# Token lists earlier and gathered tokens turned through DRAM for twelve expert jobs

## The chip, the cores and the metric

The kernel runs on one core of one Trainium2 chip. The metric is the device time of one execution in microseconds (us); it is given as the median of the runs. A profile is one further execution, recorded instruction by instruction.

## The reference

The computation is a transformer block with a mixture of experts, on 16 sequences of 256 tokens with 256 channels, all in float32. Attention has 16 heads of 64 channels; its result is added to `x`. Then each of 8 experts chooses its 512 best of the 4096 tokens (by the softmax over experts of a gate), and the chosen tokens go through that expert's two-layer network and are added back with the gate as weight:

```
shift = silu(t) @ W_ada.T + b_ada
h = ln(x, ln1_g, ln1_b) + shift
q, k, v = heads(h @ Wqkv.T);  q = ln(q, qn_g, qn_b);  k = ln(k, kn_g, kn_b)
x = x + (softmax(q @ k.T / sqrt(64)) @ v) @ Wout.T
tok = x.reshape(-1, 256)
gate = softmax(tok @ Wgate.T)
vals, idx = top_k(gate.T, 512)                  # for each of the 8 experts
g = ln(tok[idx], mlp_g, mlp_b)
y = gelu(g @ fc1s[e].T + b1s[e])                # 256 -> 1024
y = y @ fc2s[e].T + b2s[e]                      # 1024 -> 256
tok[idx] += y * vals                            # for every expert
```

## The kernel before

The span has three parts. The attention stage (0 to about 800 us) treats the 16 sequences in an order that is written out by hand. In it the turned keys and probabilities already go through DRAM: VectorE turns 32x32 blocks (L746, L832), SyncE's queue writes the blocks to DRAM (`away`) and reads them back in four transfers in another order of blocks (`back`). Then a first routing (about 800 to 850 us) chooses tokens, and an expert stage follows (about 850 us to the end).

The expert stage has 16 jobs of 256 tokens each. Jobs 0 to 7 are the eight experts with a first routing over 30 of the 32 tiles of 128 tokens; jobs 8 to 15 are the experts again with a second routing over all 32 tiles, which runs beside jobs 1 to 6. Job 0 and the lists of jobs 0 and 1 belong to the ordered part. From job 1 on a loop `for k in range(1, len(jobs))` goes through 16 slots a job; the order of its calls is the order of the instructions on each engine.

For the running job `a` (number k):

- slots 0 to 7: `up(s)` makes one eighth of the hidden layer on TensorE (L1268), `gelu(s)` applies the activation on ScalarE (L1275); `weigh` in slot 7 multiplies the bias with the tokens' weights on VectorE (L1292)
- slots 8 to 15: `down` (L1284), four slots for each 128 tokens, with `finish` on VectorE (L1295) and `scatter` (L1301) in slots 11 and 15. The scatter is an indirect DMA from GpSimd's queue (POOL) that adds rows of the output in DRAM.

For the next job `new` (k + 1), in the same slots:

- slot 5 (`LIST_AT`): `list_matmul` (L1224) turns the token list out of one-hot matrices, `take` (L1233, L1235) brings it to SBUF as indices and weights, and `gather` (L1240) fetches the normalised token rows from DRAM into `xg`, as two indirect DMAs on POOL
- slot 14 (`TURN_AT`): `transposes` (L1249) turns the gathered tokens with four TensorE matmuls into PSUM tile `px`, and `evict` (L1256) brings them to `xT` with two affine ScalarE passes (gain and bias of the layer norm)

For the job after that (`far`, k + 2): `lay_out` is a generator. It has 15 steps: the first makes `gives` (L1192, L1197), each of the 14 others two or three of the 32 one-hot matrices on VectorE (L1216). One step is taken a slot, in slots 6 to 15 of one job and 0 to 4 of the next. At the end of a job, `far.load()` puts the expert's weights on SyncE's queue: `w2` and `w1`, 1 MB each, and `b2`, 128 KB. Their buffers come free when job k has used its own.

Job 8 is the first of the second routing. In loop k = 7 its one-hots are made in slots 0 to 5, and its list in slot 7 (`LATE_AT`, the name `late`).

The second routing is a search by two bits a round. `compare_three` (L1042) counts on VectorE how many gates reach three candidates, `count_three` (L1049) adds the counts over partitions on TensorE, and `choose_bits` (L1055 to L1064) decides. A round stands in every fifth slot; `masks`, `scans`, `place` and `split` follow in loop k = 6.

Buffers that matter: `xg` has 5 ("xs"), `xT` 2 ("hT"), the one-hot tiles 2 ("kT"), and the PSUM tiles of `px` and of the routing's counts share 3 ("mm").

Of the kernel before, what the change touches and what calls it, by code (L numbers as in the profile page):

```python
# [9 lines left out]
F32 = mybir.dt.float32  # L10
I32 = mybir.dt.int32
BF16 = mybir.dt.bfloat16
AF = mybir.ActivationFunctionType
# [5 lines left out]
P = 128  # L19
# [8 lines left out]
DC = D // P  # L28
# [3 lines left out]
KL = KC // 2  # L32
CAPL = CAP // 2
NV = 5
SQ = 32
QB = P // SQ
# [3 lines left out]
LN1_G, LN1_B, B_ADA, MLP_G, MLP_B = 0, 2, 4, 6, 8  # L40
# [4 lines left out]
class Plan:  # L45
# [7 lines left out]
    def step(self, place, engine, took, run, needs=(), makes=(), tiles=(), mode=0, lag=0.1):  # L53
        k = len(self.steps)
        self.steps.append((place, engine, took, run, needs, tiles, mode, lag))
        for m in makes:
            self.makers.setdefault(m, []).append(k)
# [7 lines left out]
def kernel(  # L65
# [14 lines left out]
    nc = tc.nc  # L80

    const = ctx.enter_context(tc.tile_pool(name="const", bufs=1))
    dram = ctx.enter_context(tc.tile_pool(name="dram", bufs=1, space=DRAM))
# [6 lines left out]
    vec = const.tile([P, NVEC], F32, name="vec")  # L90
# [432 lines left out]
    if True:  # L523
        attw = ctx.enter_context(tc.tile_pool(name="attw", bufs=1))
        seq = ctx.enter_context(tc.tile_pool(name="seq", bufs=2))
        work = ctx.enter_context(tc.tile_pool(name="work", bufs=2))
# [22 lines left out]
        class Shift:  # L549
            def __init__(self):  # L550
                self.pa = {}
# [75 lines left out]
        class First:  # L627
# [22 lines left out]
            def evict(self):  # L650
                b = self.b
                hTs[b] = seq.tile([P, DC, N], F32, tag="hT", name=f"hT{b}")
                for c in range(DC):
                    nc.scalar.activation(
                        hTs[b][:, c, :], self.pt[:, c, :], AF.Identity,
                        bias=bias1[:, c, b : b + 1],
                        scale=vec[:, LN1_G + c : LN1_G + c + 1],
                    )
# [12 lines left out]
        class Group:  # L671
# [74 lines left out]
            def turn(self, kb):  # L746
                if self.t == 0:
                    kb.append(work.tile([P, QB, TB, HP // 2, SQ], F32, tag="pb", bufs=3, name="kb"))
                nc.vector.transpose(
                    kb[0][:, :, self.t],  # L750
                    self.qk.rearrange("p (h q d) -> p q h d", q=QB, d=SQ),
                )

            def away(self, kb):
                self.blocks = dram.tile([QB, SQ, QB, N], F32, tag="blocks", bufs=4, name="kblocks")
                nc.sync.dma_start(
                    self.blocks.rearrange("k d q n -> (k d) (q n)"),
                    kb[0].rearrange("p q t h m -> p (q t h m)"),
                )

            def back(self):
                kT = self.keys()[:, self.g - 2].rearrange("p k t h m -> p k (t h m)")
                for q in range(QB):
                    nc.sync.dma_start(
                        kT[bass.ts(q, SQ)], self.blocks[:, :, q].rearrange("k d n -> d k n")
                    )

            def affine(self):
                kT = self.keys()[:, self.g - 2].rearrange("p k t h m -> p (k t h m)")
                nc.scalar.activation(  # L770
                    kT, kT, AF.Identity,
                    bias=vec[:, KN_B : KN_B + 1], scale=vec[:, KN_G : KN_G + 1],
                )
# [398 lines left out]
        class Job:  # L1172
            def __init__(self, e, routing, tiles):
                self.e, self.routing, self.tiles = e, routing, tiles
                self.oh = None

            def load(self):


                e = self.e  # L1180
                self.w2 = seq.tile([P, FC, D], F32, tag="oT", name="w2")
                nc.sync.dma_start(self.w2, fc2T[e].rearrange("(f p) d -> p f d", p=P))
                self.w1 = seq.tile([P, DC, DD], F32, tag="v", bufs=2, name="w1")
                nc.sync.dma_start(self.w1, fc1T[e].rearrange("(c p) f -> p c f", p=P))
                self.b2 = moe.tile([P, D], F32, tag="b2", bufs=2, name="b2")
                nc.sync.dma_start(self.b2, b2s[:, bass.ts(e, D)].to_broadcast([P, D]))
# [66 lines left out]
            def evict(self):  # L1253
                self.xT = seq.tile([P, DC, CAPL], F32, tag="hT", name="xT")
                for c in range(DC):
                    nc.scalar.activation(  # L1256
                        self.xT[:, c, :], self.px[:, c, :], AF.Identity,
                        bias=vec[:, MLP_B + c : MLP_B + c + 1],
                        scale=vec[:, MLP_G + c : MLP_G + c + 1],
                    )  # L1260
                self.hid = seq.tile([P, FC, CAPL], F32, tag="qT", name="hid")
                self.y = work.tile([P, KL, D], F32, tag="pr", bufs=PRB, name="y")
                self.ph, self.py = {}, {}

            def up(self, f):
                self.ph[f] = ps.tile([P, CAPL], F32, tag="sc", bufs=4, name="ph")
                for c in range(DC):
                    nc.tensor.matmul(  # L1268
                        self.ph[f], self.w1[:, c, bass.ts(f, P)], self.xT[:, c, :],
                        start=(c == 0), stop=(c == DC - 1),  # L1270
                    )

            def gelu(self, f):
                k = B1 + self.e * FC + f
                nc.scalar.activation(  # L1275
                    self.hid[:, f, :], self.ph[f], AF.Gelu_apprx_tanh,
                    bias=vec[:, k : k + 1], scale=1.0,
                )

            def down(self, i, a=0, b=FC):  # L1280
# [51 lines left out]
        for b in range(B):  # L1332
# [16 lines left out]
            for (g, t), p in GROUP.items():  # L1349
                p += base  # L1350
                a = Group(b, g, t)
                n = (b, g, t)
# [23 lines left out]
            for d in range(HP // 2):  # L1376
                a = Quad(b, d)
                p = base + d * QUAD
                g = d // 2
                n = (b, d)  # L1380
                po = ("po", 0) + n
                for i in range(2):
                    q = p + 3 * i
                    m = n + (i,)
                    sums, pb, prT, blocks = ("sums",) + m, ("pb",) + m, ("prT",) + m, ("blocks",) + m
# [20 lines left out]
            for t in range(TB):  # L1406
                a = Tail(b, t)
                p = base + TAIL[t]
                n = (b, t)
# [55 lines left out]
        for n in range(2):  # L1465
            a = jobs[n]
            k = top + 10 + 20 * n
# [4 lines left out]
            for i in range(6):  # L1472
                name, took, by = {"D": ("DVE", 0.81, nc.vector), "P": ("POOL", 1.4, nc.gpsimd), "A": ("ACT", 3.5, nc.scalar)}[who[i]]
# [13 lines left out]
        k = top + 30  # L1487
# [9 lines left out]
        for k in plan.order(PLACES):  # L1497
            plan.steps[k][3]()

        LIST_AT, TURN_AT, LATE_AT = 5, 14, 7  # L1500
        SLOTS = 2 * FC

        def second_routing():
# [9 lines left out]
        def lay_out(job):  # L1513

            job.gives()
            for a in list(range(0, 18, 2)) + list(range(18, NT, 3)):
                yield
                job.onehot(a, a + (2 if a < 18 else 3))

        rest = second_routing()  # L1520
        last = len(jobs) // 2 - 2
        jobs[2].load()
        parts = iter(())
        for k in range(1, len(jobs)):
            a = jobs[k]
            new = jobs[k + 1] if k + 1 < len(jobs) else None
            far = jobs[k + 2] if k + 2 < len(jobs) else None
            late = k == last + 1
            for s in range(SLOTS):
                for step in next(rest, ()):  # L1530
                    step()
                if late and s == 0:
                    new.gives()
                if late and s < 6:
                    new.onehot(6 * s, 6 * s + 6)
                if new and s == (LATE_AT if late else LIST_AT):
                    for _ in () if late else parts:
                        pass
                    new.list_matmul(0, NT)
                    new.take()  # L1540
                    new.gather()
                    if k == 1:
                        jobs[0].scatter(by_end[1])
                if new and s == TURN_AT:
                    new.transposes()
                    new.evict()
                if not late and s < LIST_AT:
                    next(parts, None)
                if far and k != last and s > LIST_AT:
                    if s == LIST_AT + 1:  # L1550
                        parts = lay_out(far)
                    next(parts)
                if s < FC:
                    a.up(s)
                    a.gelu(s)
                    if s == FC - 1:
                        a.weigh()
                else:
                    i, q = divmod(s - FC, 4)
                    a.down(i, 2 * q, 2 * q + 2)  # L1560
                    if q == 3:
                        a.finish(i)
                        a.scatter(i)
            if far:
                far.load()
# [50 lines left out]
```

## Time and profile before

| | |
|---|---|
| time, median of 3 runs | 1104.54 us (1104.27, 1104.54, 1107.28) |
| profiled execution | 1106.04 us, of which its span is 1104.2 us |
| TensorE clock granted, mean | 0.99 |
| expert loop, k = 1 to 15 | 865.61 to 1094.80 us of the span |
| one job of k = 1 to 5 | 15.4 us |
| job k = 6 | 17.0 us |
| one job of k = 7 to 14 | 15.1 us |

The names of the engines in the profile: PE is TensorE (PEld its weight loads), DVE VectorE, ACT ScalarE, POOL GpSimd, SP SyncE (SPq its DMA issues). Times in a line of the timeline are the start in us of the span and the length in us. What stands in brackets is how long the engine was idle before the instruction and which instruction or DMA, by tile and line, ended the wait.

### The profile page before, as it was taken

The numbers are of one execution on the slowest core, as the hardware profiler recorded it, in microseconds if no ns is written. First come the engines' busy times: TensorE is split into PE (matmuls) and PEld (weight loads), VectorE is DVE, ScalarE is ACT, GpSimd is POOL, SyncE is SP. The second block draws the span as 40 slices with busy tenths as digits, with TensorE's granted clock in tenths as the row PEclk, the third lists the DMA queues.
The fourth block names the chain that finished last, engine by engine and source line by source line (L and its number), as shares of the span: only waits on it lengthen the run. The fifth ranks groups of instructions, "written<-read, shape, count | busy, mean of one in ns | idle before, by whom it ended". The sixth has DMA issues, their size and how long they took to land. (4 is left out here: it accounts for less than half of the span.)

```text
span 1104.2 us, 18872 instructions
## 1 busy us (share of the span) xinstructions
PE 1070.6 (97%) x5835; PEld 714.8 (65%) x5835; DVE 778.9 (71%) x2201; ACT 596.1 (54%) x1656; POOL 616.2 (56%) x997
## 2 busy tenths in 40 slices
PE   7999999999999999999899999999988999999996
PEld 4555656566565655656465655656767888888885
DVE  6657888777778777786678787676568488654540
ACT  2768666565766566566557667576522333322331
POOL 3766776776676665675657666565411233333332
PEclk9999999999999999999999999999999999999998
DMA  6013998785888787796787778895130456555661
GB/s 211 1 39 123 277 259 237 230 255 166 248 260 227 226 246 234 201 260 211 211 251 227 228 224 240 243 256 179 63 102 20 113 189 200 170 162 175 196 201 19
DMA packets 147539, 209.20 MB, mean 189 GB/s; under 512 B 15088, under 2 KB 122864, under 8 KB 147440
## 3 DMA queue, kind: packets, MB, share of 16 engines
q1 hardware_dynamic: 139520, 197.71, 60.0%
q0 software_dynamic: 6144, 8.39, 4.1%
q10 hardware_dynamic: 1776, 1.90, 0.5%
q8 instruction: 47, 0.77, 0.3%
q14 instruction: 52, 0.43, 0.1%
HBM read 121.96 MB, written 85.98 MB: 188 GB/s over the span
## 5 line engine op out<-in xcount | busy, mean ns | idle before, releaser
L683 PE MATMUL pm<-wq,hT 128*128 128x512 f32 x768 | 360.4, 605 | 5.0 <-DVE qk L716 2.8
L822 POOL TENSOR_SCALAR pr<-pr,sums 128x256 f32<-128x256 f32 x512 | 237.1, 481 | 112.2 <-DVE sums L818 92.9
L811 ACT ACTIVATE pr<-sc,nmax 128x256 f32<-128x256 f32 x512 | 238.0, 480 | 97.5 <-DVE nmax L802 80.3
L683 PEld LDWEIGHTS pm<-wq,hT 128*128 128x128 f32 x768 | 137.3, 192 | 146.1 <-issue 131.1
L103 POOL TENSOR_TENSOR ss<-ss,neghalf 128x8 f32<-128x8 f32 x128 | 210.5, 1645 | 10.6
L802 DVE TENSOR_REDUCE nmax<-sc 128x2 f32<-128x512 f32 x256 | 165.3, 676 | 16.9 <-PE sc L794 16.3
L832 DVE STREAM_TRANSPOSE pb<-pr 128x512 f32<-128x512 f32 x224 | 149.9, 690 | 18.5 <-POOL pr L822 13.6
L794 PE MATMUL sc<-kT,qT 64*128 64x256 f32 x1024 | 135.4, 397 | 0.0
L881 PE MATMUL po<-prT,v 128*64 128x256 f32 x1024 | 127.6, 388 | 1.1 <-DVE gates L950 1.1
L700 DVE TENSOR_REDUCE ss<-sq 128x8 f32<-128x512 f32 x128 | 86.0, 672 | 47.3 <-ACT sq L696 46.8
L794 PEld LDWEIGHTS sc<-kT,qT 64*128 64x128 f32 x1024 | 92.8, 188 | 40.8 <-issue 25.4
L696 ACT ACTIVATE sq<-pm 128x512 f32<-128x512 f32 x128 | 76.9, 603 | 77.3 <-PE pm L683 75.9
L1301 POOL DMA_INDIRECT out<-y,idx x32 | 51.2, 1601 | 119.8 <-DVE y L1295 66.9
L1268 PE MATMUL ph<-xT,w 128*128 128x256 f32 x512 | 117.6, 383 | 0.0
L907 PE MATMUL pw<-wo,oT 128*128 128x256 f32 x512 | 116.6, 381 | 0.3 <-DVE qk L716 0.3
L1284 PE MATMUL py<-w,hid 128*128 128x256 f32 x512 | 116.3, 380 | 0.0
L716 DVE TENSOR_TENSOR qk<-pm,ss 128x512 f32<-128x512 f32 x128 | 87.0, 681 | 36.9 <-POOL ss L103 35.9
L907 PEld LDWEIGHTS pw<-wo,oT 128*128 128x128 f32 x512 | 96.0, 190 | 23.2 <-issue 9.4
L811 ACT ACTIVATION_READ_ACCUMULATOR pr<-sc,nmax 128x1 f32 x512 | 107.6, 210 | 0.0
L881 PEld LDWEIGHTS po<-prT,v 128*64 128x64 f32 x1024 | 67.1, 137 | 61.5 <-issue 21.1
L1275 ACT ACTIVATE hid<-ph,vec 128x256 f32<-128x256 f32 x128 | 60.4, 474 | 84.2 <-PE ph L1268 76.3
L1284 PEld LDWEIGHTS py<-w,hid 128*128 128x128 f32 x512 | 95.6, 190 | 12.8
(140 smaller groups left out, 1132.6 us busy)
## 6 DMA issues: line engine op xcount, KB each, us to landing
blocks<-pb SPq DMA_DIRECT2D x112, 512.0 KB
prT<-blocks SPq DMA_DIRECT2D x448, 128.0 KB
w<-in_fc2T SPq DMA_DIRECT2D x16, 1024.0 KB
w<-in_fc1T SPq DMA_DIRECT2D x16, 1024.0 KB
kblocks<-kb SPq DMA_DIRECT2D x28, 512.0 KB
kT<-kblocks SPq DMA_DIRECT2D x112, 128.0 KB
out<-tok SPq DMA_DIRECT2D x32, 128.0 KB
xn_dram<-tn SPq DMA_DIRECT2D x32, 128.0 KB
```

Of the source, the lines that this page charges most:

```text
L103: nc.gpsimd.tensor_tensor(dst, src, neghalf[:, : src.shape[1]], ALU.pow)
L683: nc.tensor.matmul(self.pm, hTs[self.b][:, c, bass.ts(self.t, P)], wq[:, c, bass.ts(self.g, GW)], start=(c == 0), stop=(c == DC - 1),)
L716: engine.tensor_tensor(self.qk.rearrange("p (h d) -> p h d", d=HD), src.rearrange("p (h d) -> p h d", d=HD), self.ss[:, 1, :].unsqueeze(2) ...
L794: nc.tensor.matmul(self.sc[i, j][:, t, :], qTs[self.b][rows, hp, bass.ts(t, P)], keys[rows, hp] if direct else keys[rows, hp // 4, hp % 4] ...
L802: nc.vector.tensor_reduce(self.nmax[i, j], self.sc[i, j], AX.X, ALU.max, negate=True)
L811: nc.scalar.activation(self.pr[i, j][:, t, :], self.sc[i, j][:, t, :], AF.Exp, bias=self.nmax[i, j][:, t : t + 1], scale=1.0, accum_out=se ...
L822: nc.gpsimd.tensor_scalar(self.pr[i, j][:, t, :], self.pr[i, j][:, t, :], self.sums[i][:, 1, j, t : t + 1], 1.0, ALU.mult, ALU.mult,)
L832: nc.vector.transpose(self.pb[i][:, :, :, j].rearrange("p k c t n -> p t k c n"), self.pr[i, j].rearrange("p t (k c m) -> p t k c m", c=TB ...
L881: nc.tensor.matmul(self.po[j * HD : (j + 1) * HD, i, :], vs[self.b][:, c, bass.ts(4 * self.d + 2 * i + j, HD)], prT[:, j, c] if self.b in ...
L907: nc.tensor.matmul(self.pw, oTs[self.b][:, hp // 2, self.t, hp % 2, :], wo[:, hp, :], start=(hp == 0), stop=(hp == HP - 1),)
L1268: nc.tensor.matmul(self.ph[f], self.w1[:, c, bass.ts(f, P)], self.xT[:, c, :], start=(c == 0), stop=(c == DC - 1),)
L1284: nc.tensor.matmul(self.py[i], self.hid[:, f, bass.ts(i, P)], self.w2[:, f, :], start=(f == 0), stop=(f == FC - 1),)
```

## The change

The list of the next job moves from slot 5 to slot 0. Two jobs keep theirs: loop k = 1 (slot 5) and loop k = 7 (slot 7). In loops k = 2 to 6 and 8 to 14, twelve in all, the gathered tokens are no longer turned by TensorE. In slot 6 VectorE turns them in 32x32 blocks into `xb` (two instructions), SyncE writes `xb` to DRAM (256 KB) and reads it back in four transfers of 64 KB in the order of blocks that makes `xT`; in slot 12 ScalarE applies the two affine passes in place. The tokens of such an `xT` lie in another order, so `up` reads it through a view, and `gelu` writes the hidden layer through one that puts the tokens in their old order. The one-hots now stand in slots 1 to 15, and loop k = 1 takes two steps a slot, in slots 6 to 15.

```diff
+            def turn(self):
+                self.xb = work.tile([P, QB, DC, KL, SQ], F32, tag="prT", bufs=4, name="xb")
+                for i in range(KL):
+                    nc.vector.transpose(
+                        self.xb[:, :, :, i].rearrange("p q c m -> p c q m"),
+                        self.xg[:, i].rearrange("p (c q d) -> p c q d", c=DC, d=SQ),
+                    )
+
+            def away(self):
+                self.blocks = dram.tile([QB, SQ, QB, P], F32, tag="xblocks", bufs=2, name="xblocks")
+                nc.sync.dma_start(
+                    self.blocks.rearrange("k d q n -> (k d) (q n)"),
+                    self.xb.rearrange("p q c i m -> p (q c i m)"),
+                )
+
+            def back(self):
+                self.xT = seq.tile([P, QB, DC, KL, SQ], F32, tag="hT", name="xT")
+                xT = self.xT.rearrange("p k c i m -> p k (c i m)")
+                for q in range(QB):
+                    nc.sync.dma_start(
+                        xT[bass.ts(q, SQ)], self.blocks[:, :, q].rearrange("k d n -> d k n")
+                    )
+
+            def affine(self):
+                for c in range(DC):
+                    xT = self.xT[:, :, c].rearrange("p k i m -> p k (i m)")
+                    nc.scalar.activation(
+                        xT, xT, AF.Identity,
+                        bias=vec[:, MLP_B + c : MLP_B + c + 1],
+                        scale=vec[:, MLP_G + c : MLP_G + c + 1],
+                    )
+                self.outputs()
...
                     nc.tensor.matmul(
-                        self.ph[f], self.w1[:, c, bass.ts(f, P)], self.xT[:, c, :],
+                        self.ph[f], self.w1[:, c, bass.ts(f, P)],
+                        self.xT[:, :, c].rearrange("p k i m -> p k (i m)") if self.exchanged else self.xT[:, c, :],
                         start=(c == 0), stop=(c == DC - 1),
                     )
...
+                dst, src = self.hid[:, f, :], self.ph[f]
+                if self.exchanged:
+                    dst = dst.rearrange("p (i k m) -> p k i m", i=KL, m=SQ)
+                    src = src.rearrange("p (k i m) -> p k i m", i=KL, m=SQ)
                 nc.scalar.activation(
-                    self.hid[:, f, :], self.ph[f], AF.Gelu_apprx_tanh,
-                    bias=vec[:, k : k + 1], scale=1.0,
+                    dst, src, AF.Gelu_apprx_tanh, bias=vec[:, k : k + 1], scale=1.0
                 )
...
-        LIST_AT, TURN_AT, LATE_AT = 5, 14, 7
+        LIST_AT, TURN_AT, LATE_AT = 0, 14, 7
+        EXCHANGE = {6: ("turn", "away", "back"), 12: ("affine",)}
...
             late = k == last + 1
+            list_at = LATE_AT if late else 5 if k == 1 else LIST_AT
+            exchanged = k > 1 and not late
             for s in range(SLOTS):
...
-                if new and s == (LATE_AT if late else LIST_AT):
+                if new and s == list_at:
...
-                if new and s == TURN_AT:
+                if new and exchanged:
+                    new.exchanged = True
+                    for what in EXCHANGE.get(s, ()):
+                        getattr(new, what)()
+                elif new and s == TURN_AT:
                     new.transposes()
                     new.evict()
-                if not late and s < LIST_AT:
+                if not late and s < list_at:
                     next(parts, None)
-                if far and k != last and s > LIST_AT:
-                    if s == LIST_AT + 1:
+                if far and k != last and s > list_at:
+                    if s == list_at + 1:
                         parts = lay_out(far)
-                    next(parts)
+                    for _ in range(2 if k == 1 else 1):
+                        next(parts, None)
```

More of the change, by code (lines that the diff above doesn't have):

```diff
@@ L1175, in __init__ @@
                 self.oh = None
+                self.exchanged = False
             def load(self):
@@ L1260, in evict, with outputs @@
                     )
+                self.outputs()
[27 more added lines that the diff above has]
+                    )
+                self.outputs()
+            def outputs(self):
                 self.hid = seq.tile([P, FC, CAPL], F32, tag="qT", name="hid")
```

## The prediction

> **What bounds the kernel now.** I read the page's busy times first, then a table of windows cut at the jobs' first `up` matmuls, then the timeline of one job, then the waits and landings of the gathers. On the page:
>
> ```profile
> PE 1070.6 (97%) x5835; PEld 714.8 (65%) x5835; DVE 778.9 (71%) x2201; ACT 596.1 (54%) x1656; POOL 616.2 (56%) x997
> ```
>
> TensorE is busy 97% of the span, so only fewer TensorE instructions, or a gap on it, can move the end. The windows are loop passes k=2, 5, 6 and 8. The columns are window, length, busy time and count of PE, PEld, DVE, ACT, POOL, granted clock, DMA share, GB/s:
>
> ```profile
> 881.04:896.47 15.43, 15.43 (x103) 13.36 (x102) 12.95 (x77) 4.82 (x10) 5.16 (x4) 1.00 0.63 184
> 927.35:942.72 15.37, 15.37 (x103) 13.35 (x101) 13.65 (x84) 4.81 (x10) 5.20 (x4) 1.00 0.64 182
> 942.72:959.68 16.96, 16.60 (x111) 14.49 (x110) 8.55 (x39) 4.81 (x10) 5.19 (x4) 1.00 0.58 165
> 974.83:989.97 15.14, 15.14 (x102) 13.35 (x101) 7.84 (x40) 4.81 (x10) 5.23 (x4) 1.00 0.61 184
> ```
>
> PE fills its jobs (length 15.4 in k=1 to 5, 16.96 in k=6, 15.14 from k=7 to 14). DVE is nearly as full in k=2 to 5 (12.95, 12.93, 13.15, 13.65), where it carries the second routing, and half empty from k=8. Call T the start of a job's first `up`. The timeline of k=8 (T = 974.83; start, length, engine, line, instruction, idle before and its releaser):
>
> ```profile
> 974.83 4.48 PE L1268 MATMUL ph<-xT,w 128*128 128x256 f32 x20
> 975.02 0.37 SPq L1182 DMA_DIRECT2D w<-in_fc2T  x1
> ...
> 976.54 1.62 POOL L1301 DMA_INDIRECT out<-y,idx  x1 [3.02 <-DVE oh L1216]
> ...
> 979.14 0.95 PE L1224 MATMUL pls<-give,oh 128*128 128x10 bf16 x32
> ...
> 980.56 1.02 POOL L1240 DMA_INDIRECT xg<-xn_dram,idx  x1 [2.41 <-DVE idx L1233]
> ...
> 981.88 0.98 POOL L1240 DMA_INDIRECT xg<-xn_dram,idx  x1 [0.30 <-issue]
> ...
> 987.04 1.62 POOL L1301 DMA_INDIRECT out<-y,idx  x1 [4.17 <-DVE y L1295]
> ...
> 987.80 0.60 PE L1249 MATMUL px<-ident,xg 128*128 128x128 f32 x4
> ...
> 988.50 1.02 ACT L1256 ACTIVATE xT<-px,vec 128x256 f32<-128x256 f32 x2 [5.20 <-PE px L1249]
> ...
> 989.97 4.48 PE L1268 MATMUL ph<-xT,w 128*128 128x256 f32 x20
> ```
>
> The second gather starts at T+7.05, and `px` needs it at T+13: six us of cover, which the change spends. How much of it the landing takes (us, gathers of the jobs), and how full the DMA engines are from T+2, T+8 and T+9:
>
> ```profile
> DMA to landing us min/median/max: 2.8/3.0/4.3
> ```
> ```profile
> 976.83:977.83 1.00, 1.00 (x6) 0.89 (x5) 1.00 (x6) 0.61 (x2) 1.00 (x1) 1.00 0.95 323
> 982.83:983.83 1.00, 1.00 (x6) 0.89 (x5) 0.42 (x4) 0.47 (x1) 0.03 (x1) 1.00 0.93 276
> 983.83:984.83 1.00, 1.00 (x7) 0.87 (x6) 0.00 (x0) 0.00 (x0) 0.00 (x0) 1.00 0.24 78
> ```
>
> The expert weights, issued at T+0.2, fill the engines (shares .95, .93) until about T+9, and the gather lands at T+7.05 + 2.8 to 4.3 = T+9.9 to T+11.3: when that traffic has drained.
>
> **What is removed.** In twelve jobs the four PE transposes and the PSUM eviction go. A job of k=8 to 14 is 15.14; its 64 up/down matmuls take 64 x .2158 = 13.81 and its 32 list matmuls .81 by their spacing, so the transposes are worth 15.14 - 13.81 - .81 = .52. Twelve jobs: 6.2 us, the ceiling of the gain. The evictions were on an ACT that is busy 4.8 of 15: nothing.
>
> **What is added to DVE, and its wait.** Two 32x32-block transposes of 128x256 come to DVE; the attention stage's 128x512 one takes .69, so about .32 each, .64 a job (.9 if half of the cost is per instruction). The price is the place: slot 6, about T+6 to T+8 on PE, and DVE does its queue in order. Will the gather be there? Listing in slot 0 moves its issue: behind the former job's second scatter (starts T+1.7 now, about T+2.1 in shorter jobs, 1.6 long, .3 to the next) the gathers can start at T+4.0 and T+5.3. Their landing need not move with it. In the trace's packet records the scatter issued at T+1.7 has its packets run only at T+6.5 to T+8.5, behind weights queued before it, and the gather's run right behind it, T+8.0 to T+9.4, with stragglers to T+11. An earlier issue finds the same queue. Bounds of "xg ready": T+5.3 + 2.9 = T+8.2 if the landing moves with the issue, T+11.3 if nothing moves. I take T+10.2 (today's median landing is 7.05 + 3.0), being nearest to the packet rows.
>
> By the Trainium skill's page "DMA: Bandwidth & Descriptors", section "Queues, rings and completion order", each DMA engine alternates between its queues packet by packet, so a gather need not wait for the weights; that gives T+8.2 and a sum of +4.2 where the row gives +9.4. The packet rows above, a scatter waiting three us or more beside a full weights queue, speak against it, and I go by them.
>
> *k=2 to 5.* I laid the changed order of DVE's instructions (take, gives, one-hots and routing rounds, turn, the rest) against the durations above. DVE reaches the turn at T+6.1, 10.2, 7.8 and 8.2 (late in k=3, still behind from k=2); xg is there at T+10.2, 10.3, 10.5 and 11.4 (2.9 after an issue that late one-hots delay). It waits 4.1, .1, 2.7 and 3.2 = 10.1 in all. Queued behind the turn are the one-hots that the next list matmuls in slot 0 need, and the routing rounds, whose counts PE waits for. So DVE sets the pace: 12.95 + 12.93 + 13.15 + 13.65 = 52.7, plus 4 x .64 = 2.6, plus 10.1 = 65.4, against 61.7 now (15.43 + 15.43 + 15.45 + 15.37): +3.7 with no other idle time on DVE. It idles 9.0 there now; I leave it .6 of that for waits on PE's counts: +4.3. PE loses it in list matmuls and routing counts. *k=6* (turn reached at T+9.7): wait 1.2 + turn .64 - .52 = +1.3. First half: **+5.6**. *k=1* keeps its list in slot 5 and lays out two pieces a slot: nothing, since its DVE is busy 9.5 of 15.4.
>
> *k=8.* k=7 builds its own late list until slot 7, so of the next lay-out's 15 steps (gives, then 14 pieces of one-hots) only eight fit in slots 8 to 15. In the order of the changed kernel 18 one-hots then stand on DVE between the last `finish` and the `take`, ahead of the list matmul in slot 0 (it had five slots of cover before). At .165 each that is 2.97 of an empty PE; less .52: **+2.45**.
>
> *k=9 to 15.* One-hots are done in time, DVE has room. What is late is the exchange. It is unlike anything in this stage; the attention stage's is the nearest row (SyncE's issues: 512 KB away, then back in four):
>
> ```profile
> 68.99 0.34 SPq L756 DMA_DIRECT2D kblocks<-kb  x1
> 71.63 1.76 SPq L764 DMA_DIRECT2D kT<-kblocks  x4
> ```
>
> Half the bytes: some 2.0 until `back` may issue (2.64 there), 1.76 of issues, 1.4 to the last data: 5.2, with engines then free of weights. Bounds 4.2 (issues shorter) and 6.1 (as there). The SP queue holds only this job's weights before it, and waiting in it delays the next weights by less than a job's end. So xT's first half is ready at T + 10.2 + .64 + 5.2 + .56 (first affine pass, as long as the eviction's pass) = T+16.6, and `up` of the next job wants it at T + 14.62 + .81 = T+15.43 (the period without transposes, and the list): a stall of 1.2. Stalled jobs end later while their gather, which hangs on the list before the stall, does not, so the job behind has 1.2 of slack and the stalls alternate. Three or four stalls in seven jobs, 3.6 to 4.8, less 6 x .52 = 3.1: +.5 to +1.7; with three and most of a fourth (.8, at k=15) I take **+1.3**.
>
> The strided `up` operand I cost at nothing: the attention scores (L794) read exchanged keys by the same kind of view, and their median, 376 ns, is also their minimum. The permuted gelu output gets up to .1 a pass (128x256 ACT passes take .47 to .56 here), under an ACT that is two thirds idle.
>
> **Sum.** 5.6 + 2.45 + 1.3 = +9.4. The profiled execution took 1106.04 (span 1104.2, 1.84 around it), 1.5 above the median of the runs, 1104.54. The additions are the same for both: 1115.4 profiled, **1113.9** in the runs. The landing decides the size: the same walk gives +4.2 at T+8.2, +6.7 at T+9.4, +13.2 at T+10.9. A slower exchange (6.1) gives +3 more, a dearer turn (.9) +1.2. A gap can also halve PE's clock for a while: after PE had been busy in part at 800 to 804 came
>
> ```profile
> 806.00:808.00 2.00, 2.00 (x12) 1.61 (x13) 0.92 (x6) 0.73 (x2) 0.00 (x0) 0.50 0.05 12
> ```
>
> 3.4 us at .5, 1.7 lost. The gap at k=8 may be long enough.
>
> **The rivals.**
> *The landing moves with the issue* (T+8.2). For it: both gathers are behind one scatter and nothing else on POOL, and the landing after issue is nearly constant, 2.8 to 4.3. Against: the packet rows. DVE's wait in k=2 shrinks to 2.1, but from k=3 on the issue itself is late, so the first half still loses 4.0 (k=2 to 5: 2.7); all but .8 of the stalls at `up` vanish; k=8 stays: 4.0 + 2.45 + .8 - 3.1 = +4.2, 1108.7.
> *The cover holds* (the other side): DVE never waits at the turn. It decides if xg has landed when DVE first gets there, T+6.1, that is .8 after the second issue. Then xT is ready at 6.1 + .64 + 5.2 + .56 = T+12.5, no `up` waits, and all twelve blocks of transposes are gained: -6.2 + 2.45 = -3.8, 1100.7. Against it: no gather of this stage landed in under 2.8.
> *All of it later*: the gather at T+10.9, the exchange slower beside stragglers, a halved clock at k=8: 13.2 + 1.7 and part of the exchange's 3: +16, 1120.5. For it: the four landings above the median, and the away and back DMAs come while scatters run.
> That the transposes stay on PE can be excluded: the changed kernel's order has them only in the jobs not exchanged.
>
> **How the numbers follow.** The forecast has .57, the early landing .18, the late one .20, full cover .05. The range reaches from below the early landing, 1107 (4.2 less the 1.7 by which the later stalls may be missing), to 1122 (the late case and a little); about 2 in 10 is left out. About .3%, or 3.3 us, is what a measurement of this kernel can tell from no change: 1101.2 to 1107.9. Faster is the full cover, .05; within it lies a piece of the early landing, .07; slower .88.
>
> **What would show it.** Right: in the profile after, the DVE transposes with idle time before them released by the gather's DMA, 3 to 4 us in k=2, 4, 5; list matmuls or routing counts of k=3 to 6 with PE idle before them; a gap of about 3 us before the list matmul of k=8; jobs of k=9 to 14 alternating near 14.6 and 15.8; the gather's issue at T+4 to T+5.3 with a landing of about 5. Wrong: a landing still near 3 us, or a DVE that reaches the turn so late that it waits for nothing. If PE has no gaps in k=2 to 8, the time will be below 1104.

## The result, and the profile after

The changed kernel takes 1146.8 us (median of 4 runs, 1141.24 to 1148.88) against 1104.4 (4 runs) for the kernel before: ratio 1.0373, 95% interval 1.0354 to 1.0391, slower by 42 us. The sign was forecast, the size was not: +9.4 was said, with a range up to 1122. The profiled run is the fastest of the four, 1141.24 us (span 1139.4), 35 us above the profiled run of before.

The page's busy times, and of the groups by line those that answer to the forecast (the last column is idle time just before, and its releaser; in the changed kernel L1305 is `up`, L1225 the list, L1049 the routing's count, L1241 the gather, L1342 the scatter, L1267 the turn, L1274 `away`, L1283 `back`, L1290 the affine passes):

```profile
PE 1084.4 (95%) x5787; PEld 720.2 (63%) x5787; DVE 784.7 (69%) x2225; ACT 596.9 (52%) x1656; POOL 616.7 (54%) x997
```
```profile
L1305 PE MATMUL ph<-xT,w 128*128 128x256 f32 x476 | 115.5, 402 | 8.5 <-ACT xT L1290 8.0
L1225 PE MATMUL pls<-give,oh 128*128 128x10 bf16 x436 | 21.0, 170 | 3.8 <-DVE oh L1217 3.5
L1267 DVE STREAM_TRANSPOSE xb<-xg 128x256 f32<-128x256 f32 x24 | 10.1, 438 | 75.8 <-DMA xg<-xn_dram,idx 75.7
L1049 PE MATMUL pc<-cnt,block 128*128 128x3 bf16 x15 | 2.5, 168 | 10.8 <-DVE reach L1042 10.8
```

VectorE waits 75.8 us for the gathers, 6.3 a job. In k = 2 to 6, where the forecast has a wait for each job, it is 2.1 to 6.2 us (20.8 in all) where .1 to 4.1 (11.3) were said; in the second half, where VectorE has room, the wait itself costs nothing, but what stands behind it is late. TensorE waits for the routing's counts (10.8), for `xT` (8.0) and for one-hots (3.5, and the list matmuls themselves are stretched, by them and by the clock, to 21.0 us busy from 13.4). The `up` matmuls are longer on average (402 ns from 383): that is the clock. Windows of k = 2, 5, 8, 11 and 12, each cut at the end of the former job's last `down` (called T from here on; in the kernel before it lies .2 us behind the prediction's T; the columns are those of the prediction), and one of 2 us:

```profile
879.50:896.83 17.33, 15.17 (x105) 12.89 (x101) 11.39 (x65) 4.37 (x10) 4.35 (x4) 1.00 0.58 188
936.32:959.92 23.60, 19.43 (x104) 16.00 (x101) 14.95 (x92) 5.98 (x12) 6.78 (x5) 0.80 0.46 139
993.57:1012.86 19.29, 18.45 (x103) 15.22 (x100) 11.37 (x60) 4.68 (x10) 5.24 (x4) 0.91 0.53 168
1045.85:1060.55 14.70, 14.70 (x103) 12.96 (x100) 7.04 (x35) 3.79 (x8) 3.74 (x4) 1.00 0.66 208
1060.55:1077.49 16.94, 15.55 (x103) 13.27 (x100) 6.75 (x37) 4.88 (x10) 5.04 (x4) 1.00 0.65 192
936.00:938.00 2.00, 1.68 (x32) 1.34 (x30) 1.90 (x15) 1.09 (x2) 1.61 (x1) 0.50 0.16 28
```

k = 5 takes 23.60 us where 15.38 stood before, and its granted clock is .80 on average; k = 2, 8 and 12 lose 1.8 to 4.2 us; k = 11 runs at the 14.70 that the missing transposes allow. The last line shows TensorE at half its clock behind a gap. That came five times (from 935.5, 956.0, 997.0, 1031.1 and 1082.3, each behind a wait of TensorE; once 6.8 us, else 3.4 us): 20.5 us at half speed, 10.2 lost. From k = 2 to 7 the loss is 20.3 us (114.1 from 93.8), from k = 8 to 15 16.6 (136.4 from 119.8); the loop of this execution began 1.7 us earlier than that of the profile before, which makes it 35.

What the forecast did not see stands in the timeline of k = 11 to 12 (T = 1060.55 for k = 12):

```profile
1060.39 1.62 POOL L1342 DMA_INDIRECT out<-y,idx  x1 [8.40 <-DVE oh L1217]
...
1061.05 0.40 SPq L1183 DMA_DIRECT2D w<-in_fc2T  x1
...
1068.95 1.58 POOL L1342 DMA_INDIRECT out<-y,idx  x1 [6.94 <-DMA out<-y,idx]
...
1070.84 1.02 POOL L1241 DMA_INDIRECT xg<-xn_dram,idx  x1 [0.30 <-issue]
1072.16 0.98 POOL L1241 DMA_INDIRECT xg<-xn_dram,idx  x1 [0.30 <-issue]
1073.72 0.45 DVE L1267 STREAM_TRANSPOSE xb<-xg 128x256 f32<-128x256 f32 x1 [9.38 <-DMA xg<-xn_dram,idx]
...
1078.67 1.62 POOL L1342 DMA_INDIRECT out<-y,idx  x1 [5.54 <-DVE oh L1217]
```

The first line is scatter(0) of job 11. It starts not at about T+12 of its job, as before, but at its end, because `finish(0)` (L1336 below) stood on VectorE behind the turn and the one-hots of the slots between, and the turn waited until 1056.2:

```profile
1056.19 0.92 DVE L1267 STREAM_TRANSPOSE xb<-xg 128x256 f32<-128x256 f32 x2 [7.27 <-DMA xg<-xn_dram,idx]
1057.03 0.70 DVE L1217 TENSOR_SCALAR oh<-lane,partf 128x128 bf16<-128x128 bf16 x4
...
1058.16 1.55 DVE L1217 TENSOR_SCALAR oh<-lane,partf 128x128 bf16<-128x128 bf16 x9
1059.63 0.48 DVE L1336 SCALAR_TENSOR_TENSOR y<-py,w,bw 128x256 f32<-128x256 f32 x1
```

So scatter(0) goes out .7 us ahead of the next 2 MB of weights. The third line of the upper timeline is scatter(1): it waits for scatter(0)'s landing and starts 8.6 us behind it (4.65 before). The gathers are behind scatter(1) and start at T+10.3 and T+11.6 where T+4.0 and T+5.3 were forecast. VectorE waits 9.4 us at the turn, and scatter(0) of this job (the last line) is late in turn. In 7 of 14 jobs the two scatters stand 5.9 to 10.2 us apart, and behind those the second gather starts at T+8.1 to T+13.4; in the five other exchanged jobs at T+5.1 to T+6.3. From issue to landing of the scatters as far as the traces have it (us), before and after:

```profile
DMA to landing us min/median/max: 3.8/3.8/3.9
```
```profile
DMA to landing us min/median/max: 3.7/4.6/9.4
```

The two rows are not of the same scatters. The trace before has hardly a landing but those of scatter(0), at T+12 and without weights beside it; the row after has scatter(1) too. A scatter(1) issued beside the weights lands late in the kernel's old order as well: 7.2 to 8.3 us in k = 2 to 7 of e10 below, which are as before. What is new is that scatter(0) is among the late ones: 5.2 to 9.4 us in seven jobs, and these are the seven with the long distance.

### The profile page after: what moved, and what is told of

Read it like the earlier page. It is cut to its first block, busy times and chain, and to the rows that moved or that the text cites. A ratio compares the mean times of both kernels' runs of the same rounds, so it can differ in the third digit from the quotient of the medians.

```text
span 1139.4 us, 18905 instructions
## 1 busy us (share of the span) xinstructions
PE 1084.4 (95%) x5787; PEld 720.2 (63%) x5787; DVE 784.7 (69%) x2225; ACT 596.9 (52%) x1656; POOL 616.7 (54%) x997
## 5 line engine op out<-in xcount | busy, mean ns | idle before, releaser
L1342 POOL DMA_INDIRECT out<-y,idx x32 | 51.1, 1597 | 181.2 <-DVE oh L1217 91.3
L1305 PE MATMUL ph<-xT,w 128*128 128x256 f32 x512 | 123.5, 401 | 8.5 <-ACT xT L1290 8.0
L1305 PEld LDWEIGHTS ph<-xT,w 128*128 128x128 f32 x512 | 99.7, 200 | 25.5 <-ACT xT L1290 10.7
## 6 DMA issues: line engine op xcount, KB each, us to landing
w<-in_fc2T SPq DMA_DIRECT2D x16, 1024.0 KB, 6.5
w<-in_fc1T SPq DMA_DIRECT2D x16, 1024.0 KB, 8.7
```

The source lines that it names most:

```text
L1305: nc.tensor.matmul(self.ph[f], self.w1[:, c, bass.ts(f, P)], self.xT[:, :, c].rearrange("p k i m -> p k (i m)") if self.exchanged else sel ...
```

## The experiments

The theory (L) is that loop: a wait on VectorE delays a scatter into the weights, its landing delays the gathers, and these make the next wait. The diffs are against the changed kernel unless it says otherwise.

**e1: the gathers ahead of scatter(1).**

```diff
                     new.gather()
+                    if held:
+                        held.scatter(1)
+                        held = None
...
-                        a.scatter(i)
+                        if i and k + 2 < len(jobs) and k not in (last, len(jobs) - 2):
+                            held = a
+                        else:
+                            a.scatter(i)
```

> Theory L (a loop through the scatters): while VectorE waits in slot 6 for the gather, finish(0) stands behind it; scatter(0) is then issued just ahead of or beside the next weights and lands in 7 to 9 us where it took 3.9; scatter(1) waits for that landing, the gathers stand behind scatter(1) on the POOL queue, and the next wait in slot 6 is longer. Here the gathers of slot 0 are issued ahead of the former job's scatter(1), which follows them. L: the loop is cut, both gathers start by T+3 in every job (T+8 to T+13 in six jobs of the change), the waits in slot 6 fall from 6.3 us a job to 4 or less, time 1108 to 1120. Rival W (the gather lands when the weights have drained, whenever it is issued, and VectorE's order does the rest): xg lands at T+10 in every job, waits in slot 6 stay at 3 to 4 us, time 1113 to 1120 if the order of the scatters was the rest, 1130 or more if it was innocent. Rival X (the way through DRAM is itself too long): the stalls at the first up, 8.5 us in all, stay, time over 1135.

1118.56 us (ratio 1.0132, 1.0106 to 1.0158): 28 of the 42 us are gone by the order of two instructions on POOL. In k = 9 to 14 the gathers start at T+1.26 and T+2.58 (in k = 3 to 6 at T+2.3 to T+5.6, behind late lists), the waits in slot 6 are 43.6 us in all, 3.6 a job. X is out, and W with the order of the scatters innocent (1130 or more) too; the time and the waits do not tell L from W with that order as the rest. In k = 12:

```profile
1048.36 1.02 POOL L1241 DMA_INDIRECT xg<-xn_dram,idx  x1 [1.59 <-DVE idx L1234]
1049.68 0.98 POOL L1241 DMA_INDIRECT xg<-xn_dram,idx  x1 [0.30 <-issue]
1050.97 1.61 POOL L1342 DMA_INDIRECT out<-y,idx  x1 [0.30 <-issue]
1055.46 0.45 DVE L1267 STREAM_TRANSPOSE xb<-xg 128x256 f32<-128x256 f32 x1 [5.39 <-DMA xg<-xn_dram,idx]
1056.30 0.45 DVE L1267 STREAM_TRANSPOSE xb<-xg 128x256 f32<-128x256 f32 x1 [0.40 <-DMA xg<-xn_dram,idx]
```

Issued beside the weights, the second gather is there at about T+9 (1056.3, when the turn that waits for it starts; T = 1047.1), 6.6 us behind its start. Issued at T+7.05 in the kernel before it landed at T+10: 4.5 us earlier in, 1 us earlier out. That part of the forecast, that the landing beside the weights hardly moves with the issue, holds.

**e2: the turn behind finish(0).**

```diff
-        EXCHANGE = {6: ("turn", "away", "back"), 12: ("affine",)}
+        EXCHANGE = {12: ("turn", "away", "back"), 15: ("affine",)}
```

> The turn moves from slot 6 to slot 12, behind finish(0) on VectorE, and the affine passes from slot 12 to slot 15. L: VectorE has nothing to wait for at the turn, finish(0) and scatter(0) are back at T+12, scatter(1) follows 4.65 us behind, the gathers start at T+4.0 and T+5.3 in every job; the price is at the next first up, where xT comes at about T+18: stalls of 2 to 3 us in every second job; time 1112 to 1122. W: the same landing, 1112 to 1122, with scatter(0) to scatter(1) still far above 4.65 in some jobs. X: the stalls at up grow to 3 us in every job, time over 1140.

1179.2 us (1.0670, 1.0647 to 1.0693): far above what L and W said, and the case of X. The loop is gone as L says: VectorE waits for nothing at the turn, the scatters stand 4.5 to 4.7 us apart in every job. But `xT` is late, by 2.6 to 5.8 us, in every job from k = 3 on but k = 8:

```profile
L1305 PE MATMUL ph<-xT,w 128*128 128x256 f32 x480 | 134.9, 448 | 45.9 <-ACT xT L1290 45.9
```

45.9 us of stalls at `up`, and one or two stretches of halved clock behind nearly each (34.1 us lost). The expected "every second job" was wrong: the turn now stands behind the stall, so it shifts with it, and no job gets slack. On SyncE's queue `back` waits for `away` ahead of the next weights and holds them up by 1.7 to 3.9 us.

**e3: the second half only** (`list_at` is 5 up to k = 6, `exchanged = k > last + 1`).

> The change is made for the seven jobs of k = 8 to 14 alone; k = 1 to 6 are those of the kernel before. L and W: the second half's part of the loss by the two profiles is 136.5 - 120.0 = 16.5 us (last 8 jobs), so 1119 to 1123, if the halves do not feed each other. If the loop is started in the first half only (where VectorE has no room), k = 9 to 14 run at 14.7 to 15.8 a job and the time is 1107 to 1110.

1126.55 us (1.0183, 1.0148 to 1.0217): +21 (16 to 24 by the interval), no less than the half's 16.6 in the profile of the change. Its jobs k = 8 to 15 take 19.5, 14.7, 16.7, 23.0, 14.7, 16.9, 20.6 and 19.1 us in the profile. So the loop starts and feeds itself where VectorE is half empty: a full VectorE is not what starts it.

**e4: the list in slot 0 alone** (`exchanged = False`).

> The list stands in slot 0 as in the change, but the tokens are turned by TensorE in slot 14 as before (no exchange). L, W and X alike: nothing waits on VectorE, scatters and gathers keep their pace, what is lost is k = 8 with its wait for 18 one-hots, 3 us, and up to 1.7 for a halved clock behind it: 1107 to 1109.5. If it is far above that, the earlier list itself does harm.

1108.48 us (1.0033, 1.0016 to 1.0050). k = 8 takes 19.87 us (15.14 before), all other jobs of the second half are unchanged. This part was priced right: 3 us of one-hots and a halved clock (1.7 lost).

**e5: the weights later** (`load` on ScalarE's queue in slot 3 of the next job, in place of SyncE's at its start).

> The order of gathers and scatters is that of the change. Only the next expert's weights are issued later: from ScalarE's queue behind gelu(2), at about T+3.4 of the next job, not from SyncE's at T+0.2. L says that a late scatter(0) does harm because it lands beside the weights; now it lands before them, in 4 to 5 us, scatter(1) follows within 5.5 us and the gathers start by T+6 in every job; they then land beside the weights, about T+10, so waits in slot 6 stay at 3 to 4.5 us: 1112 to 1125. If the weights are innocent of scatter(0)'s slow landing (another cause), scatter(1) still comes 8 to 10 us behind in several jobs and the time stays over 1138.

1160.62 us (1.0499, 1.0480 to 1.0517). The scatters now land before the weights, with all the rest of the loop in place:

```profile
DMA to landing us min/median/max: 3.7/3.9/4.2
```

So it is the weights beside them that made these landings long. The time was still missed by 35 us or more: now the gathers (up to 8.2 us to landing) and the exchange meet the weights, VectorE still waits 65.4 us at the turn, `up` stalls for 17.4 us in all, and the clock loses 23.9.

**e6: e1 with the lay-out of k = 7 at two steps a slot** (`range(2 if k == 1 or late else 1)`).

> The kernel with the gathers ahead of scatter(1), and in k = 7 two steps of the lay-out a slot in place of one, so that no one-hots are left for the start of k = 8. By the first of these runs k = 8 took 19.15 us, of it 3 us of waiting for one-hots and up to 1.7 of a halved clock: L and W expect k = 8 at 14.7 to 15.2 and the time 4 to 4.5 us below that run: 1114 to 1115. If k = 8 loses its time elsewhere, 1118.

1117.37 us (1.0107, 1.0091 to 1.0122). k = 8 takes 14.70 us (19.15 in e1), as expected; the time is not (1114 to 1115 was said). The profiled run has 18.7 to 18.8 in k = 3, 5 and 13, where e1 had 18.6 to 18.8 in k = 5 and 10, each with a halved clock. In these two executions most of what k = 8 gave came back there.

**e7: e6 with the weights behind gelu(2)** (e1, e5 and e6 together), and **e8: the same for k = 8 to 14 alone.**

> Gathers ahead of scatter(1), the spread lay-out in k = 7 and the weights behind gelu(2), together. The gathers are issued at T+1.3 and T+2.6, ahead of the weights. If the weights' traffic is what holds a gather (L and W agree), they land in about 3 us, T+5.6, VectorE waits in slot 6 for nothing, and k = 9 to 14 run at 14.65 to 14.8; the way through DRAM then runs beside the weights, 6 to 8 us, and xT is ready at T+13.5 to T+15.5: time 1099 to 1106. If the landing has its own length of 5 to 6 us, waits of 2 us stay in slot 6 and the time is 1106 to 1114. X: stalls at up of 2 us or more a job, over 1115.

> As the run with all three, but the exchange and the early list in k = 8 to 14 alone, where VectorE has room; k = 1 to 6 as in the kernel before. Seven blocks of transposes of .52 are removed, so 3.6 us is the most to gain: 1101 to 1104 if nothing waits; 1104 to 1108 if one or two stalls at up with a halved clock are left.

1134.8 us (1.0269, 1.0251 to 1.0288) and 1122.83 (1.0163, 1.0146 to 1.0180): both came out above what was expected of a working exchange, e7 in the range of X. The gathers do land early, free of the weights: the timeline of e7 has them issued at 1024.0 and 1025.3 and turned at 1026.9 and 1028.2. What then meets the weights is the exchange:

```profile
1028.62 0.34 SPq L1274 DMA_DIRECT2D xblocks<-xb  x1
1036.14 1.73 SPq L1283 DMA_DIRECT2D xT<-xblocks  x4
...
1039.62 1.09 ACT L1290 ACTIVATE xT<-xT,vec 128x256 f32<-128x256 f32 x2 [8.55 <-DMA xT<-xblocks]
1040.27 2.02 PE L1305 MATMUL ph<-xT,w 128*128 128x256 f32 x5 [2.02 <-ACT xT L1290]
```

`back` may be issued 7.5 us behind `away` (2.1 in most jobs of the change), and the exchange takes 11 us. All of this stage's chain (gather, away, back) wants the six us of a job in which no weights run.

**e9: finish(0) off VectorE.**

```diff
+            def finish_off(self, i):
+                nc.scalar.activation(self.y[:, i], self.py[i], AF.Identity, scale=self.w[:, i : i + 1])
+                nc.gpsimd.tensor_tensor(self.y[:, i], self.y[:, i], self.bw[:, i], ALU.add)
...
-                    if s == FC - 1:
+                    if s == 5:
                         a.weigh()
...
-                        a.finish(i)
+                        (a.finish if i else a.finish_off)(i)
```

> The change as it is (scatter(1) ahead of the gathers, turn in slot 6, weights at T+0.2), but finish(0) leaves VectorE: ScalarE multiplies, GpSimd adds the bias, and weigh stands in slot 5, ahead of the turn. So the wait in slot 6 can no longer delay scatter(0). L in its full form (the loop runs through finish(0)): scatter(0) starts by T+13 in every job without a stall at up, scatter(1) follows 4.6 to 5 us behind it, the gathers start by T+6 except where the list itself is late, waits in slot 6 are 4 to 4.5 us, time 1112 to 1122, near the forecast of the prediction, which held this distance fixed. If the distance and the time stay as in the change (over 8 us in six jobs, 1140 and more), finish(0) is not the link.

1135.46 us (1.0280, 1.0263 to 1.0296). The link is shown: in k = 8 to 14 the scatters stand 4.6 to 5.5 us apart (6.6 and 6.7 in two jobs of the first half) and the second gather starts by T+6.9 in every exchanged job. But only 11 us come back, and the time lies 13 us above the end of what L expected. The jobs now alternate as the forecast had it, with larger numbers: 14.7 and 19.3 to 20.6 where 14.65 and 15.8 were said (k = 11 and 12):

```profile
1037.85:1052.56 14.71, 14.71 (x104) 12.97 (x100) 7.14 (x36) 4.27 (x9) 6.35 (x5) 1.00 0.68 209
1052.56:1071.88 19.32, 16.93 (x103) 14.41 (x100) 8.74 (x48) 6.31 (x13) 5.90 (x5) 0.91 0.62 182
```

GpSimd's addition itself moves the gathers back by 1.3 us (T+6.5 from T+5.2 in these jobs), which adds to the stalls at `up`: 12.4 us in all, and 10.2 are lost to the clock. How much of the 42 us belongs to the loop alone is thus left between about 11 (here, with that addition as a cost of its own) and 28 (e1, which also issues the gathers earlier); no run cuts the loop and nothing else.

**e10, e11, e12: the best versions.** e10 is e6 for k = 8 to 14 alone. In e11 `w1` of the next weights, whose buffer is free after the last `up`, goes right behind `back` on SyncE's queue; e12 is e11 for all twelve jobs.

```diff
                         a.weigh()
+                        if far and exchanged:
+                            far.early = True
+                            far.load_w1()
```

> Exchange and early list in k = 8 to 14 alone, gathers ahead of scatter(1), lay-out of k = 7 at two steps a slot, weights on SyncE's queue at T+0.2. In the run with the same for all twelve jobs these jobs took 14.7 to 15.5 us with one of 18.7 (a stall and a halved clock). All theories: 1103 to 1109, about the time of the kernel before; nothing is gained as long as xT comes at T+15.1 to T+15.5, just when up wants it.

> As the run beside it, but the half of the next weights whose buffer is free early (w1, 1 MB) is put on SyncE's queue right behind the four back transfers (about T+13.4), so that only w2 and b2 (1.1 MB) go at T+0.2 of the next job. If the weights' traffic is what holds the gathers (W as part of L), it ends 1.5 to 4 us earlier, the gathers land by T+6.5, xT is ready by T+13.7, k = 9 to 14 run at 14.65 to 14.75 without a stall, and the time is 1100.5 to 1103. If w1 beside the tail of back and scatter(0) costs more than it frees, over 1106.

> The same for all twelve jobs. The first half keeps a VectorE with 13 us of work and two turns of .45 each in jobs of 14.7; with xg at T+6.5 its waits in slot 6 vanish, and what is left is work: 13.2 + .9 = 14.1 us a job. L: 1100 to 1106. If the first half stays at 15.3 to 18.8 a job as with the gathers first, 1108 to 1113.

1107.02 us (1.0020, 1.0006 to 1.0034), 1105.51 (1.0005, 0.9995 to 1.0016) and 1113.22 (1.0068, 1.0053 to 1.0083). e10 is as expected; e11 lies between its two expectations, e12 at the upper end of its second. In e11 k = 11 to 14 run at 14.70 each with the second gather landed by T+8.4 and `xT` in time. One hitch (in the profile k = 9: `away` takes 4.1 us to land where it takes 2.0 elsewhere, just behind a late scatter(1), then k = 10 is at 18.94 with a halved clock) costs more than the seven blocks of transposes bring, and the time is that of the kernel before. None of the versions tried beats it; in e12 the first half keeps two jobs of 18.8 and 21.6.

**e13: no weights loaded from job 3 on.**

> The change with one cost taken away: from job 3 on the jobs' w1 and w2 are not loaded; they use those of jobs 1 and 2 over again (so the outputs of those jobs are of other experts' weights), b2 is still loaded. If the weights' traffic is what makes every other transfer slow, the loop has nothing to live on: scatter(0) to scatter(1) 4.6 to 4.8 us in every job, gathers at T+4.0 and T+5.3 and landed by T+8.3, xT ready by T+14.5, no stall at up in k = 9 to 14 (14.65 a job); what is left is VectorE's waits in slot 6 of 2 us in k = 2 to 6 and k = 8 with its late one-hots: 1104 to 1112. If the landings are slow of themselves (X, or a queue's own length), they stay at 5 us and more and the time at 1125 or more.

1117.86 us (1.0119, 1.0090 to 1.0148), 29 below the change. The scatters:

```profile
DMA to landing us min/median/max: 3.7/3.8/5.1
```

The gathers land in 2.7 to 4.2 us. So the weights' traffic stands behind the larger part, 29 of the 42 us; as gathers and exchange run without it too, this does not single out the loop. The time is 6 us above the end of what was expected. Left are waits on VectorE (43.7 us in slot 6), lists in slot 0 that wait for one-hots, 4.2 us of waits for `xT` at `up`, and 3.4 us of the clock: scatter(1) still starts at T+2.4 to T+3.8 in k = 9 to 14, behind a `finish(1)` or a scatter(0) that the turn made late.

**e14: the kernel before, with finish(0) and scatter(0) in slot 15** (ahead of finish(1) and scatter(1)).

> The kernel before (list in slot 5, turn on TensorE), with one edit: finish(0) and scatter(0) move from slot 11 to slot 15, ahead of finish(1) and scatter(1). It makes the link of the loop by hand, without an exchange and without a wait on VectorE: scatter(0) at T+15 stands just ahead of the next weights. L: scatter(1) follows not 4.65 but 8 to 10 us later, the gathers, now behind it, start at T+9 to T+12 in place of T+5.7 and T+7.0, land after T+13, and TensorE waits for px: 1.0 to 3 us a job, 1120 to 1150. If scatter(0) lands in 4 to 5 us there too, the gathers start by T+7 and the time is 1104 to 1108.

1116.48 us (1.0104, 1.0062 to 1.0147): +11 from late scatters, with no exchange anywhere. POOL from k = 1 on:

```profile
877.45 1.56 POOL L1301 DMA_INDIRECT out<-y,idx  x1 [6.17 <-DVE y L1295]
887.99 1.57 POOL L1301 DMA_INDIRECT out<-y,idx  x1 [8.99 <-DMA w<-in_fc1T]
889.87 1.02 POOL L1240 DMA_INDIRECT xg<-xn_dram,idx  x1 [0.30 <-DVE reach L1042]
```

scatter(0) goes out at the end of k = 1 beside the weights, scatter(1) follows 10.5 us later, and the gather, which the kernel before starts at T+5.6 there, starts at T+12.9. (The second line's wait is put down to a weight load; scatter(0)'s own landing, 9.8 us behind its start, comes .7 us ahead of scatter(1), much as in the late pairs of the change.) TensorE waits 7.4 us for gathered tokens in all, and the clock, halved three times, loses 6.8. scatter(0) came late in k = 1 to 6 only, which is why the time stays under the expectation: from k = 7 on VectorE is free when `py` is ready, and finish(0) runs at its old time though it stands later in the order.

## Why the prediction was wrong

- **What was right.** TensorE set the time, and what counts is gaps on it. A removed block of transposes is worth .44 (jobs of 14.70 from 15.14; .52 was said). In the jobs with a gather at T+5.1 to T+5.3 the turn begins at T+9.5 to T+10.4 (T+10.2 said), and from its end to the first affine pass it takes 5.5 to 6.2 us (5.2 said; 8.0 in k = 8). The turn takes .44 an instruction (.32 said, .45 was the upper bound). The 18 one-hots of k = 8 came as said (e4, e6). The Trainium skill's page "DMA: Bandwidth & Descriptors" (section "Queues, rings and completion order") has the queues take turns packet by packet, by which the gather was put at T+8.2; e1's second gather, issued 2.7 us sooner still, is there at T+9. In k = 8 of the trace before, the packets of the scatter and the gather do run side by side with those of the weights, but only from T+6.5 on; by the measurement a gather beside the weights waits all the same.
- **The step that failed** is "the gathers can start at T+4.0 and T+5.3". It moved the second scatter along with the job (T+1.7 to T+2.1), which holds only as long as scatter(0) keeps its place at T+12 and scatter(1) its 4.65 us behind it. The prediction had listed what is queued behind the turn on VectorE as one-hots and routing rounds; `finish(0)` is queued there too, and through it scatter(0), scatter(1) and the next gathers. In seven of twelve exchanged jobs the second gather started at T+8.1 to T+13.4. A landing of 3.8 to 3.9 us was taken as a property of the scatter, when it was one of its place, at a time without weights; the prediction's own packet rows had a scatter beside the weights run five us behind its issue, and it did not ask whether scatter(0) could come to stand there. e1, e5, e9, e13 and e14 each show a link of this.
- **The terms.** The first half (k = 2 to 6) was put at +5.6 and lost 18.9; k = 7 at nothing, and lost 1.4; k = 8 at +2.45, and lost 4.2 (1.7 of it the clock); k = 9 to 15 at +1.3, and lost 12.4. Of the first half 10.8 us are TensorE's waits for the routing's counts, whose instructions on VectorE stand behind the turn.
- **Mis-sized.** The halved clock was priced once, 1.7 us, in one rival; it came five times, 10.2. A gap of 1.2 to 1.7 us at `up`, forecast as such, can cost 1.7 more.
- **Rivals.** "All of it later" (+16) had the right side and the wrong reason; the loop was in none. The range could not hold it, since each bound was taken with the others fixed.

## What to carry to other kernels

When a change puts a wait into an in-order queue, go round once: list every instruction behind it, the DMAs that these release, and what those hold up, until you are back at the wait. If you come back, the cost is not the wait but the loop. A landing time in a trace belongs to its place in the traffic; before a transfer is moved, look at what runs where it will land, and find the part of the period in which the large transfers do not run: here it was six us, and gather, exchange and scatter all want it.

## What the runs showed of the hardware that was not expected

- An indirect DMA or a 256 KB write issued beside 2 MB of weights, on another queue, takes two to four times as long: scatters 3.8 to 9.4 us (9.8 in e14, 10.3 in e7), gathers 2.8 to 6.5 (8.2 in e5), `away` 2.0 to 8.5 (e7).
- The clock is halved for 3.4 us (once for 6.8) after gaps as short as 1.2 us (1080.5 to 1081.7, halved from 1082.3) and 1.7 us (1028.3 to 1030.0, halved from 1031.1), in e1 even behind one of .6 us (930.65 to 931.27, halved from 931.7). Other gaps of 1.1 (1062.2) and 1.9 us (1098.8) were followed by none. So the length of the gap alone does not decide, and what does is not shown here. A stall of this size costs 0 or 1.7 us more, and which of them the trace before could not tell. Two windows of the change, one with the gap of 1.7 us and one at half the clock:

```profile
1028.00:1030.00 2.00, 0.35 (x14) 0.25 (x11) 1.93 (x12) 0.63 (x2) 0.05 (x1) 1.00 0.94 121
1032.00:1034.00 2.00, 2.00 (x7) 1.55 (x6) 0.00 (x0) 0.47 (x1) 1.56 (x1) 0.50 1.08 392
```
